# A down projection as seven block products: ten of eleven weight chunks multiplied by blocks, weights streamed by block, angle tables moved to DRAM

## The chip, the cores and the metric

The kernel runs on one core of one Trainium2 chip. The metric is the device time of one execution in microseconds; the time of a kernel is the median over its runs. A core has five engines that run side by side, each with its own in-order queue: TensorE (PE in the profile, its weight loads PEld), VectorE (DVE), ScalarE (ACT), GpSimd (POOL) and SyncE (SP), which only issues transfers (DMAs) and waits. An engine waits at an instruction until the semaphores that it needs have arrived, and all that stands behind it on that engine waits too.

## The reference, cut to what matters

Four layers follow each other on 2048 rows of 512 numbers, all in fp32. Layer 0 is a feed-forward with experts, layer 2 attention over a paged cache, layer 3 a short mix at the end. The change lies in layer 1, apart from a table that layer 2 uses. With `x` the result of layer 0, `F` = 1376 and rank 16, layer 1 computes:

```python
def lora_add(base, inp, A, B):          # a low-rank part for each sequence, of rank 16
    t = einsum('bri,bni->bnr', A[ids], inp)
    return base + einsum('bor,bnr->bno', B[ids], t) * 0.5

gate = lora_add(x @ W_gate.T, x, A_gate, B_gate)     # 512 -> 1376
up   = lora_add(x @ W_up.T,   x, A_up,   B_up)
act  = silu(gate) * up
down = lora_add(act @ W_down.T, act, A_down, B_down) # 1376 -> 512, this product changes
x = x + adapters(down)                               # a base product and gated adapters
```

Layer 2 rotates queries and keys by angles: `cos(pos * freq)` and `sin(pos * freq)`, for each of the 2048 positions 64 numbers.

## The kernel before, in words

The kernel is written in a tile framework: the code names tiles and operations, and the framework sets semaphores, hands out buffers and puts the instructions of each engine in an order. A tile name with `bufs=n` has n buffers; a new tile of that name waits until the readers of the tile n before it are done. Where the code wants an order of its own it adds edges:

- `on_pe` ties each matmul to the one before it, so TensorE's order is that of the program.
- `load_by` ties each of its loads on SP to the one before it, so these loads too go out in program order. An entry that waits for a buffer or for data holds up all that follow.
- the gathers of layer 1 (`gather`, on POOL) are put behind `last_sum`, the last store of a weight sum.

Layer 1 goes over eight groups of 256 rows (two tiles of 128). A group has two phases. First come the *features*: gate and up for eleven chunks of F, ten of 128 and one of 96 (`FC`, `NFC` = 11). They are already computed as seven block products in place of eight (`p1` to `p7`), on sums of the weights and sums of x, with matmuls of 128 columns. `seconds` adds the low-rank part, two chunks at a time, and `finish` makes `actT` on ACT and DVE. In chunk f, `p7(f)` puts a product into the accumulator `acc_a`, DVE reads it at line 587, and `p4(f)` then overwrites it, so TensorE waits for that read.

Second comes the *down phase*: `down` multiplies the eleven chunks of `actT` by `down1T`, four matmuls of 256 columns for each chunk. The down tiles are loaded by `next_down`, seven ahead (`AHEAD`); a product frees a buffer for the tile seven further. Between chunks ten and eleven stand the low-rank products `low` (for the next group, `low_ps`) and `low_down` (`low_d_ps`). Two copies, on ACT and DVE, bring the result `pz` to `zT`, which the adapters (`choose`, `base`, `out`) use during the features of the next group.

Beside this POOL prepares layer 2: `all_sums` yields pairs of functions. `rows` loads four blocks of a weight matrix (`blocks`, two buffers) through `load_by`; `add` makes four sums of them on POOL and stores them to DRAM. Layer 2 reads them as weights of its own block products. Each group makes five sums, one function for each feature chunk (`parts`).

So SP's program order in a group is: rows of the first two sums (chunks 0 and 2), then `load_firsts` for the low-rank weights of down and of the next group's x (16 loads, and register loads ahead of each eight), rows of the third sum, the seven down tiles, the x of the next group, rows of the last two sums, and in the down phase the remaining down tiles. The next group's x is turned by TensorE in the last feature step, just ahead of the down phase.

`rotary_tables` makes cos and sin once, while layer 0 runs, and keeps both in SBUF (4 KB of each partition apiece) up to the end of layer 2, where POOL multiplies them with norm weights in `tables`.

Of the kernel before, what the change touches and what calls it, by code (L numbers as in the profile page):

```python
# [24 lines left out]
F32 = mybir.dt.float32  # L25
I32 = mybir.dt.int32
U32 = mybir.dt.uint32
AF = mybir.ActivationFunctionType
ALU = mybir.AluOpType
# [4 lines left out]
P = 128  # L34
B, S, D = 64, 32, 512
NT = B * S // P
# [4 lines left out]
F1 = 1376  # L41
FC = [(o, min(P, F1 - o)) for o in range(0, F1, P)]

# [308 lines left out]
def sum_up(c, pool, blocks, dst):  # L352


    nc = c.nc
    w = []

    def rows():
        w.append(pool.tile([P, 4, D // 2], F32, name="blocks", bufs=2))
        for n, block in enumerate(blocks):  # L360
            c.load_by(w[0][:, n, :], block)

    def add():
        t = pool.tile([P, 4, D // 2], F32, name="sums")
        (b11, b12, b21, b22), (t1, t2, t3, t4) = ([v[:, n, :] for n in range(4)] for v in (w[0], t))
        nc.gpsimd.tensor_tensor(t1, b12, b11, ALU.subtract)
        nc.gpsimd.tensor_tensor(t3, b22, b12, ALU.subtract)
        nc.gpsimd.tensor_tensor(t2, b22, t1, ALU.subtract)
        nc.gpsimd.tensor_tensor(t4, b21, t2, ALU.subtract)
        c.last_sum = nc.gpsimd.dma_start(dst, t).ins  # L370

    return rows, add
# [10 lines left out]
def all_sums(c, pool, sums):  # L383

    a, H = c.a, D // 2
    for h in range(HALVES):
# [14 lines left out]
def layer1(c, kp, x_in, x_out, sums):  # L401
# [14 lines left out]
    AHEAD = 7  # L416
    with ExitStack() as ctx:
# [34 lines left out]
        class Group:  # L452
            def __init__(self, g):
                self.g = g
                self.h, self.po = [None] * G, [None] * G
                self.a, self.b, self.c, self.part, self.first, self.wd = {}, {}, {}, {}, {}, []
# [166 lines left out]
            def next_down(self, f):  # L623

                if f < NFC:
                    w = FC[f][1]
                    t = wdp.tile([P, D], F32, name="down1T")
                    c.load_by(t[:w], a["down1T"][f * P:f * P + w])
                    self.wd.append(t)

            def down(self, fs, last):
                if 0 in fs:
                    self.pz = [ps.tile([P, 2, N], F32, tag=tag, bufs=2, name="pz") for tag in "ab"]
                for f in fs:
                    w, wd = FC[f][1], self.wd.pop(0)
                    for m in range(KC):
                        product(self.pz[m // 2][:, m % 2, :], wd[:w, m * P:(m + 1) * P],
                                self.actT[:w, f, :], m % 2 == 0 and f == 0, False)
                    self.next_down(f + AHEAD)
                if not last:  # L640
                    return
                for m in range(KC):
                    product(self.pz[m // 2][:, m % 2, :], self.B["Bd1"][:, m * P:(m + 1) * P],
                            self.low_d[:, 0, :], False, m % 2 == 1)
                self.zT = gp.tile([P, KC, N], F32, name="zT")
                nc.scalar.copy(self.zT[:, 0:2, :], self.pz[0])
                nc.vector.tensor_copy(self.zT[:, 2:4, :], self.pz[1])
# [61 lines left out]
        wB = c.load(wp, "B1", [P, D], a["B1"])  # L709
        nb_thr = c.row(wp, "b_thr1")  # L710
# [25 lines left out]
        for g, new in enumerate(groups):  # L736
            old = groups[g - 1] if g else None
            then = groups[g + 1] if g + 1 < len(groups) else None
            parts = [f for _ in range(5) for f in next(to_sum)]

            def features(f):
# [9 lines left out]
                if f:  # L751
                    new.p4(f - 1)
                    if f % 2:
                        new.seconds(f - 1, False)
                        if f < NFC:
                            new.seconds(f, True)
                    new.finish(f - 1)
                if f < NFC:
                    new.p6(f)
                    new.p3(f)  # L760
                if g == 0:
                    sums_of(f + 2)
                if f < len(parts):
                    parts[f]()
# [33 lines left out]
            new.down(range(NFC - 1), False)  # L798
# [4 lines left out]
            new.down((NFC - 1,), True)  # L803
# [10 lines left out]
def rotary_tables(c, pool, scratch):  # L814
# [12 lines left out]
    tables = []  # L827
    for name, turn in (("cos", 0.25), ("sin", 0.0)):
# [4 lines left out]
        r = scratch.tile([P, NT, half], F32, name="rest")  # L833
# [4 lines left out]
        t = pool.tile([P, NT, half], F32, name=name)  # L838
        nc.scalar.activation(t, r, AF.Sin)
        tables.append(t)  # L840
    return tables


class Known:


    def __init__(self, c, kp):
        tc, nc, a = c.tc, c.nc, c.a
        half = HD // 2
        with tc.tile_pool(name="l2_setup", bufs=1) as scratch:  # L850
            self.cos, self.sin = rotary_tables(c, kp, scratch)
# [34 lines left out]
def attention(c, known, x_in, y_part, y_out, sums, tail):  # L886
# [18 lines left out]
    with ExitStack() as outer:  # L905
# [8 lines left out]
        cos, sin, rows, lens = known.cos, known.sin, known.rows, known.lens  # L914
# [110 lines left out]
        class Projections:  # L1025
# [10 lines left out]
            def load(self):  # L1036
                self.xt = [c.load(xp, "xt", [P, D], x_in(T), bufs=2) for T in self.T]

            def tables(self, n):
                for i, T in enumerate(self.T):  # L1040
                    ct = qp.tile([P, 2, half], F32, name=n + "_cos")
                    st = qp.tile([P, 2, half], F32, name=n + "_sin")
                    for t, w_n, f in ((ct, norm[n][0], cos), (st, norm[n][1], sin)):
                        self.last_pool = nc.gpsimd.tensor_tensor(
                            t, w_n, f[:, T, :].unsqueeze(1).to_broadcast([P, 2, half]), ALU.mult).ins
# [672 lines left out]
def emit(tc, a, layers=(0, 1, 2)):  # L1718
    with ExitStack() as ctx:
# [11 lines left out]
        for n in layers:  # L1731
# [3 lines left out]
            if n != 0 and n == next(m for m in layers if m):  # L1735
# [3 lines left out]
                known = Known(c, kp)  # L1739
                sums = {}  # L1740
                for h in range(HALVES):
# [95 lines left out]
```

## Time and profile before

| | us |
|---|---|
| median of 3 runs (3495.23 to 3498.11) | 3495.39 |
| the profiled execution, device time | 3498.47 |
| its span, first to last instruction | 3496.7 |
| TensorE busy in it | 3432.7 (98%) |
| DVE / ACT / POOL busy in it | 2124.5 / 1554.7 / 1617.2 |
| features of group 0, then its down phase | 376.8 to 423.6, to 447.2 |
| features of a later group (602.7 to 657.6), its down phase | 54.9, 23.4 |

Layer 0 ends and layer 1 begins near 374 us of the span, layer 1 ends near 1006, layer 2 near 3327.

How the views are read: a timeline row has the start in us, the length in us, the engine, the line of the kernel, the operation, output<-inputs by the program's names, the shape and the count of merged instructions; in brackets stands how long the engine had been idle before and what released it. A matmul in fp32 shows as two records. `SPq` is SP's queue of transfers; the length is that of the issue, not of the transfer. Matmuls overlap, so their pace is the distance of starts and not the length.

### The profile page before, as it was taken

What the parts mean: (1) busy time and instruction counts of PE and PEld (TensorE: products, weight loads), DVE (VectorE), ACT (ScalarE), POOL (GpSimd) and SP (SyncE); (2) the same over time, 40 slices, a digit from 0 to 9 for tenths busy, and PEclk for the clock granted to TensorE, in tenths of its full rate; (3) what the DMA queues carried; (4) which work ended last, traced back from release to release, by engine and by line L of the source; (5) the groups of instructions that cost most, each with busy time, mean ns of one, the idle gap of its engine ahead of it and who ended that gap; (6) DMA issues with size and microseconds to landing.
All of it is one profiled execution on the core that took longest, in us unless ns stands there. A gap on an engine that the chain in (4) does not pass through costs nothing. (4 is left out here: it accounts for less than half of the span.)

```text
span 3496.7 us, 65764 instructions
## 1 busy us (share of the span) xinstructions
PE 3432.7 (98%) x20736; PEld 2601.2 (74%) x20736; DVE 2124.5 (61%) x5284; ACT 1554.7 (44%) x4089; POOL 1617.2 (46%) x1606
## 2 busy tenths in 40 slices
PE   8999999999999999999999999999999999999999
PEld 4445788888856778777787787777877778778755
DVE  4443534434457676766767767677676676766433
ACT  4111222222226555655555555555565555555411
POOL 0112432323336645645556455465564655644232
PEclk9999999999999999999999999999999999999999
DMA  6013454544466788888878888878888788887721
GB/s 220 25 34 126 159 168 154 168 151 157 139 202 213 239 261 251 259 258 256 257 249 258 255 250 258 262 251 267 256 260 262 247 267 250 259 259 241 228 85 58
DMA packets 630635, 736.00 MB, mean 210 GB/s; under 512 B 64274, under 2 KB 480018, under 8 KB 630290
## 3 DMA queue, kind: packets, MB, share of 16 engines
q1 hardware_dynamic: 577810, 558.74, 51.4%
q0 software_dynamic: 50176, 168.86, 13.9%
q8 instruction: 168, 2.75, 0.3%
q10 hardware_dynamic: 2304, 4.20, 0.3%
q14 instruction: 177, 1.45, 0.1%
HBM read 689.61 MB, written 41.94 MB: 209 GB/s over the span
## 5 line engine op out<-in xcount | busy, mean ns | idle before, releaser
L957 POOL DMA_INDIRECT vt<-in_v_rows,v_rows x512 | 512.5, 1001 | 304.9 <-PE po L931 178.7
L1220 ACT ACTIVATE pr<-pr,low 128x544 f32<-128x544 f32 x512 | 383.3, 749 | 532.3 <-DVE low L1218 486.0
L1213 PE MATMUL sc<-kt,qT 128*128 128x288 f32 (+1 forms) x2048 | 555.5, 394 | 8.1 <-DVE low L1218 6.5
L931 PE MATMUL po<-prT,vt 128*128 128x128 f32 x4096 | 544.9, 276 | 7.4 <-ACT prT L1231 5.9
L931 PEld LDWEIGHTS po<-prT,vt 128*128 128x128 f32 x4096 | 522.7, 192 | 39.1 <-ACT prT L1231 19.0
L1213 PEld LDWEIGHTS sc<-kt,qT 128*128 128x128 f32 x2048 | 385.1, 190 | 223.1 <-issue 123.0
L1218 DVE CUSTOM_DVE_ANT_0 pr<-sc,mask 128x544 f32<-128x544 f32 x512 | 368.2, 719 | 139.3 <-PE sc L1213 101.5
L1005 POOL TENSOR_TENSOR projected<-projected,swapped 128x512 f32<-128x512 f32 x160 | 208.4, 1302 | 300.9 <-DVE projected L1004 277.8
L1225 DVE TENSOR_SCALAR pr<-pr,low 128x512 f32<-128x512 f32 x512 | 315.3, 616 | 12.8
L926 PE MATMUL prT_ps<-ident,pr 128*128 128x128 f32 x2048 | 311.7, 275 | 2.6 <-DVE pr L1225 2.4
L1231 ACT COPY prT<-prT_ps 128x512 f32<-128x512 f32 x512 | 294.0, 574 | 35.2 <-PE prT_ps L926 20.1
L1222 DVE RECIPROCAL low<-low 128x1 f32<-128x1 f32 x512 | 82.0, 160 | 312.8 <-ACT pr L1220 245.7
L926 PEld LDWEIGHTS prT_ps<-ident,pr 128*128 128x128 f32 x2048 | 237.4, 142 | 11.8 <-issue 3.8
L931 PE MATMUL py<-wo,oT 128*128 128x256 f32 x1024 | 241.8, 379 | 0.0
L931 PE MATMUL pq<-wp,x_sums 128*128 128x512 f32 x512 | 240.8, 593 | 0.9 <-issue 0.5
L931 PEld LDWEIGHTS py<-wo,oT 128*128 128x128 f32 x1024 | 186.5, 190 | 21.1
L130 POOL TENSOR_TENSOR rs<-rs,minus_half 128x4 f32<-128x4 f32 x160 | 181.0, 1131 | 22.5 <-DVE low L1222 14.9
L931 PE MATMUL pq<-wp,xT 128*128 128x512 f32 x384 | 182.0, 597 | 3.9 <-DVE projected L1091 3.9
L931 PE MATMUL py<-wo,o_sum 128*128 128x256 f32 x768 | 181.4, 380 | 4.4 <-DVE o_sum L1149 2.5
L1223 ACT ACTIVATE own_pr<-pr,low 128x32 f32<-128x32 f32 x512 | 164.9, 322 | 46.2 <-DVE low L1222 37.4
L1006 POOL TENSOR_TENSOR projected<-projected,rs 128x512 f32<-128x512 f32 x160 | 172.4, 1078 | 7.9
L964 ACT COPY own_vt<-v 32x128 f32<-32x128 f32 x512 | 150.8, 295 | 54.9 <-PE po L931 42.4
(283 smaller groups left out, 6197.7 us busy)
## 6 DMA issues: line engine op xcount, KB each, us to landing
kt<-in_kT SPq DMA_DIRECT2D x2048, 64.0 KB
wp<-in_sums SPq DMA_DIRECT2D x192, 512.0 KB
wo<-out_sums SPq DMA_DIRECT2D x128, 512.0 KB
wp<-in_WqT SPq DMA_DIRECT2D x96, 512.0 KB
wo<-in_WoT SPq DMA_DIRECT2D x96, 512.0 KB
down1T<-in_down1T SPq DMA_DIRECT2D x80, 256.0 KB
wp<-in_WkT SPq DMA_DIRECT2D x32, 512.0 KB
xt<-x SPq DMA_DIRECT2D x48, 256.0 KB
```

What stands on the lines that cost most here:

```text
L130: self.nc.gpsimd.tensor_tensor(t, t, self.minus_half[:, :n], ALU.pow)
L926: c.on_pe(nc.tensor.transpose(pt[:, m, :], piece, c.ident))
L931: c.on_pe(nc.tensor.matmul(out, lhsT, rhs, start=first and i == 0, stop=last and i == len(pairs) - 1))
L957: nc.gpsimd.indirect_dma_start(out=vts[b % 2][:, n, :], out_offset=None, in_=a["v_rows"], in_offset=bass.IndirectOffsetOnAxis(ap=rows[h][: ...
L1005: nc.gpsimd.tensor_tensor(src, src, tmp, ALU.add)
L1006: nc.gpsimd.tensor_tensor(src, src, rs.unsqueeze(2).to_broadcast([P, REP, HD]), ALU.mult)
L1213: c.on_pe(nc.tensor.matmul(sc[:, lo + n * PSIZE:lo + m * PSIZE].rearrange("p (n k) -> p n k", k=PSIZE), q, kt[:, n:m, g, :], start=True, s ...
L1218: nc.vector.tensor_tensor_reduce(pr[:, :NK], sc[:, lo:lo + NK], masks[h, b], -SCALE, 3.0e38, ALU.add, ALU.min, low[:, 0:1])
L1220: nc.scalar.activation(pr[:, :NK], pr[:, :NK], AF.Exp, bias=low[:, 0:1], scale=-1.0, accum_out=low[:, 1:2])
L1223: nc.scalar.activation(own_prs[b % 2][:, g * S:(g + 1) * S], pr[:, L:NK], AF.Copy, scale=low[:, 2:3])
L1225: nc.vector.tensor_scalar(pr[:, :L], pr[:, :L], low[:, 2:3], None, ALU.mult)
L1231: last_prT.append(nc.scalar.copy(prT, pt).ins)
```

## The change

The first ten chunks of the down product become a 2x2 block product by the same scheme as the features: the K side is cut into chunks 0 to 4 and 5 to 9 (`FB` = 5), the rows into the two tiles of the group, the 512 outputs into two halves. Each half again is made in two steps `u` of 128 outputs. For each `u` seven products of five chunks, with 128 columns each, take the place of eight; the order is `DOWN`. Four of the seven use sums of the weights, which `all_sums` now makes first and stores to `down_sums` in DRAM: five more sums, all in group 0, which makes ten where the others make five. Four sums of activations are made on DVE after `finish` of chunks 5 to 9 (`act_sums`). The weights of a product are one tile of five blocks of 128x128, 14 tiles a group, five ahead. The eleventh chunk (`wd_last`, now loaded once) and the low-rank part are added in `down_rest`, which also makes `zT` out of the blocks. To fit in SBUF, `blocks` has one buffer instead of two, and the angle tables go to DRAM, from where layer 2 loads 64 KB for each tile of rows.

```diff
     def rows():
-        w.append(pool.tile([P, 4, D // 2], F32, name="blocks", bufs=2))
+        w.append(pool.tile([P, 4, D // 2], F32, name="blocks"))
...
 def all_sums(c, pool, sums):
     a, H = c.a, D // 2
+    for f in range(FB):
+        yield sum_up(c, pool, [a["down1T"][at * P:(at + 1) * P, n * H:(n + 1) * H] for at in (f, f + FB)
+                               for n in range(2)], sums["down"][:, f])
...
-    AHEAD = 7
+    AHEAD = 5
+    DOWN = (1, 5, 6, 7, 2, 3, 4)
...
+            def act_sums(self, i):
+                x11, x21 = (self.actT[:, i, t * P:(t + 1) * P] for t in range(2))
+                x12, x22 = (self.actT[:, i + FB, t * P:(t + 1) * P] for t in range(2))
+                if i == 0:
+                    self.s = gp.tile([P, 4, FB, P], F32, name="act_sums")
+                s1, s2, s3, s4 = (self.s[:, n, i, :] for n in range(4))
+                nc.vector.tensor_tensor(s1, x21, x22, ALU.add)
+                nc.vector.tensor_tensor(s2, s1, x11, ALU.subtract)
+                nc.vector.tensor_tensor(s3, x11, x21, ALU.subtract)
+                nc.vector.tensor_tensor(s4, x12, s2, ALU.subtract)
+
+            def next_down(self, i):
+                if i < 2 * len(DOWN):
+                    u, m = i // len(DOWN), DOWN[i % len(DOWN)]
+                    t = wdp.tile([P, FB, P], F32, name="down1T")
+                    if m in (1, 2, 3):
+                        k, n = {1: (0, 0), 2: (1, 0), 3: (1, 1)}[m]
+                        at = (2 * n + u) * P
+                        src = a["down1T"][k * FB * P:(k + 1) * FB * P, at:at + P].rearrange("(f p) n -> p f n", p=P)
+                    else:
+                        src = sums["down"][:, :, {5: 0, 6: 1, 7: 2, 4: 3}[m], u * P:(u + 1) * P]
+                    c.load_by(t, src)
                     self.wd.append(t)
...
+            def down(self, u, ms):
+                lo, hi = slice(0, FB), slice(FB, 2 * FB)
+                for m in ms:
+                    if m in (1, 2):
+                        t = ps.tile([P, D], F32, tag="a" if m == 1 else "b", bufs=2, name="pz")
+                        self.pz[u, m == 2] = t.rearrange("p (n c) -> p n c", n=4)
+                    x = {1: self.actT[:, lo, :P], 2: self.actT[:, hi, :P], 4: self.actT[:, hi, P:],
+                         3: self.s[:, 3], 5: self.s[:, 0], 6: self.s[:, 1], 7: self.s[:, 2]}[m]
+                    at, w = {1: 0, 6: 1, 7: 2, 5: 3, 2: 0, 3: 1, 4: 2}[m], self.wd.pop(0)
+                    for f in range(FB):
+                        product(self.pz[u, m in (2, 3, 4)][:, at, :], w[:, f, :], x[:, f, :],
+                                m in (1, 2) and f == 0, f == FB - 1, more=m not in (1, 2))
+                    self.next_down(u * len(DOWN) + DOWN.index(m) + AHEAD)
+
+            def down_rest(self, u):
+                pz = self.pz[u, True].rearrange("p (t n) c -> p t n c", t=2)
+                w = FC[-1][1]
+                for n in range(2):
+                    q = slice((2 * n + u) * P, (2 * n + u + 1) * P)
+                    for lhsT, rhs in ((wd_last[:w, q], self.actT[:w, NFC - 1, :]), (self.B["Bd1"][:, q], self.low_d[:, 0, :])):
+                        product(pz[:, :, n, :], lhsT, rhs.rearrange("p (t c) -> p t c", t=2), False, True, more=True)
...
+                pa, v = self.pz[u, False], tp.tile([P, 5, P], F32, name="pz_sums", bufs=1)
+                nc.scalar.copy(v[:, 0], pa[:, 0])
+                nc.vector.tensor_tensor(v[:, 4], pa[:, 1], v[:, 0], ALU.add)
+                nc.vector.tensor_tensor(v[:, 2], pa[:, 2], v[:, 4], ALU.add)
+                nc.vector.tensor_tensor(v[:, 1], pa[:, 3], v[:, 4], ALU.add)
+                nc.vector.tensor_tensor(v[:, 3], pa[:, 3], v[:, 2], ALU.add)
+                nc.vector.tensor_tensor(self.zT.rearrange("p (n m) (t c) -> p m t n c", n=2, t=2)[:, u], pz,
+                                        v[:, :4].rearrange("p (t n) c -> p t n c", t=2), ALU.add)
...
-            parts = [f for _ in range(5) for f in next(to_sum)]
+            parts = [f for _ in range(5 if g else 5 + FB) for f in next(to_sum)]
...
                     new.finish(f - 1)
+                    if FB <= f - 1 < 2 * FB:
+                        new.act_sums(f - 1 - FB)
...
-                if f < len(parts):
-                    parts[f]()
+                for part in parts[:1 if g else 2]:
+                    part()
+                del parts[:1 if g else 2]
...
-            new.down(range(NFC - 1), False)
+            new.down(0, DOWN)
             if then:
                 then.x_sums()
                 then.low()
             new.low_down()
-            new.down((NFC - 1,), True)
+            new.down(1, DOWN[:4])
+            new.down_rest(0)
+            new.down(1, DOWN[4:])
+            new.down_rest(1)
...
-def rotary_tables(c, pool, scratch):
+def rotary_tables(c, scratch, dst):
...
-        t = pool.tile([P, NT, half], F32, name=name)
-        nc.scalar.activation(t, r, AF.Sin)
-        tables.append(t)
-    return tables
+        nc.scalar.activation(r, r, AF.Sin)
+        nc.sync.dma_start(dst[:, :, m, :], r)
...
                 self.xt = [c.load(xp, "xt", [P, D], x_in(T), bufs=2) for T in self.T]
+                self.angles = [c.load(xp, "angles", [P, 2, half], known.angles[:, T], bufs=4) for T in self.T]
```

## The prediction

> **What bounds the kernel now.** I read the page first, then TensorE's timeline over one steady layer-1 group, then the queue of SyncE (SP) and GpSimd (POOL) in the first group, then VectorE (DVE) beside one pair of feature chunks.
>
> ```profile
> span 3496.7 us, 65764 instructions
> PE 3432.7 (98%) x20736; PEld 2601.2 (74%) x20736; DVE 2124.5 (61%) x5284; ACT 1554.7 (44%) x4089; POOL 1617.2 (46%) x1606
> ```
>
> TensorE is busy 98% of the span: what shortens its own work shortens the kernel, and what makes it wait lengthens it by the whole wait. Its order is written out by hand (on_pe), so nothing can fill a hole.
>
> ```profile
> 579.08 17.43 PE L450 MATMUL pz<-actT,down1T 128*128 128x256 f32 x80
> 596.44 1.27 PE L450 MATMUL low_ps<-xT,first_x 128*32 128x64 f32 x64
> 597.52 1.65 PE L450 MATMUL low_d_ps<-actT,first_down 128*32 128x64 f32 x88
> 599.10 1.99 PE L450 MATMUL pz<-actT,down1T 96*128 96x256 f32 x8
> 600.93 1.89 PE L450 MATMUL pz<-low_d,Bd 128*128 128x256 f32 x8
> 602.66 0.61 PE L450 MATMUL acc_a<-xT,gate1T 128*128 128x128 f32 x4
> 603.10 0.61 PE L450 MATMUL acc_c<-x_sums,sums_gate_up 128*128 128x128 f32 x4
> ```
>
> The first column is the start, and from start to start is the pace. Each fp32 matmul of the code is two records. The ten full chunks are 40 matmuls in 17.36 us, 0.434 each with 256 columns; a run of four records with 128 columns takes 0.447, so 0.2236 a matmul. The down phase runs from 579.08 to 602.66, 23.6 us, with no wait. There are eight such groups.
>
> ```profile
> 376.98 0.33 SPq L102 DMA_DIRECT2D blocks<-in_WkT  x1
> ...
> 384.19 0.43 SPq L102 DMA_DIRECT2D blocks<-in_WvT  x1
> 388.76 5.41 SPq L102 DMA_DIRECT2D first_down<-in_A1down  x8
> 398.55 5.15 SPq L102 DMA_DIRECT2D first_x<-in_A1x  x8
> 403.80 0.37 SPq L102 DMA_DIRECT2D blocks<-in_WkT  x1
> ...
> 405.63 3.29 SPq L102 DMA_DIRECT2D down1T<-in_down1T  x7
> 408.96 0.91 SPq L102 DMA_DIRECT2D xt<-x  x2
> ...
> 425.50 5.51 SPq L102 DMA_DIRECT2D down1T<-in_down1T  x4
> ```
>
> This is group 0 on SP. load_by keeps these loads in program order, and the rows show that order: two sums' blocks, the low-rank firsts, a third sum's blocks, seven down tiles, the next x, later the other down tiles. SP passes each in time only because it rarely has to wait for POOL, which consumes the blocks:
>
> ```profile
> 384.67 0.73 POOL L366 TENSOR_TENSOR sums<-blocks 128x256 f32<-128x256 f32 x1 [5.81 <-DMA blocks<-in_WvT]
> 393.20 0.72 POOL L366 TENSOR_TENSOR sums<-blocks 128x256 f32<-128x256 f32 x1 [4.22 <-DMA in_sums<-sums]
> ```
> ```profile
> 668.75 0.72 POOL L366 TENSOR_TENSOR sums<-blocks 128x256 f32<-128x256 f32 x1 [7.28 <-DMA blocks<-in_WvT]
> 675.48 0.74 POOL L366 TENSOR_TENSOR sums<-blocks 128x256 f32<-128x256 f32 x1 [2.66 <-DMA in_sums<-sums]
> ```
>
> From one sum's first add to the next with nothing else in the way: 8.5 us while the queues are full, 6.7 later. A sum is a slow thing, and the change moves sums in front of TensorE's weights.
>
> **The change, part by part.**
>
> *Down products.* Removed: 17.36 us a group. Added: 2 output pairs x 7 products x 5 chunks = 70 matmuls at 0.2236 = 15.65. The eleventh chunk and the low-rank part stay 8 matmuls of 256 columns, 3.56 us (599.10 to 602.66), only split over u. Gain 1.71 us a group, 13.7 over eight.
>
> *Ten sums in group 0, one block buffer.* Group 0 now makes 10 sums instead of 5 (parts is 5 + FB, two parts per feature chunk), the five of down first, and blocks has one buffer: rows of sum k+1 wait on SP until the adds of sum k are done, and everything behind them on SP waits too. The next SP entries are, in order: rows 0 to 2, firsts, rows 3 and 4, down tiles 0 to 4, the next x, rows 5 to 9, down tiles 5 to 13. Tile 1 is product 5's, read from the sums in DRAM, so it waits for the store of sum 4. One sum now costs: adds 2.95 (668.75 to the end of L369), then either the store (0.3, 0.8 and 2.7) or the reload (first add 2.85 after the first issue, as from 456.96 to 459.81, and 0.4 more for the fourth block). Both give 6.3 to 6.8; I take 6.8. Then, in span time:
> - sums 0, 1, 2 start at 384.7, 391.5, 398.3; rows 2 are issued by 396.2.
> - The firsts take SP 19.2 us (384.5 to 403.7 before, register loads included): 415.4. Sum 3 starts at 418.3, sum 4 at 425.1, its adds end at 428.1 and its store has landed at 431.7.
> - SP issues tiles 1 to 4 and x until 434.3. The x tiles come behind 1.3 MB of weights; with 222 GB/s at a DMA share of 0.67 in this phase before (331 at full), they land at about 438.5. TensorE transposes this x before the down phase, at 420.58 before, so it stands from there: about 18 us.
> - It then needs 3.0 us to the down phase (420.58 to 423.58) and 5.6 for products 0 to 4: 447, a microsecond or two more after the idle time.
> - Rows 5 go out at 434.3, behind the same traffic: sum 5 at 440, sums 6 to 8 at 446.8, 453.6, 460.4, rows 9 until 465.1, tile 5 issued then and landed at 468.5. TensorE stands a second time, over 20 us.
> - What is left of the phase: 9 products 10.1, low_ps 1.1, low_d 1.6, the rests 3.6, together 16.3, and 2.0 for the clock: after the idle time at the handover of layers low_ps took 1.94 (374.86 to 376.80) against 1.08 later, and the next twelve records lost another 1.2. End 486.8, against 447.2: **+39.6 us**, group 0's own saving in it. With 6.3 a sum and tile 5 sooner it is +33, with 8.5 as at the start +50.
>
> The gathers for group 1 are put behind the last sum on POOL: about 472 to 477, wanted by the second chunk of that group near 495, so covered.
>
> In groups 1 to 7 the same queue has five sums over 78 us: the last block loads were issued by 636.4 before and slip by one sum, to about 643, while tile 5 is wanted at 658.7. That cover is 15 us, and I cost the single buffer there at nothing. Without the cover each sum too many would cost 6.8.
>
> *Sums of activations.* 20 VectorE adds of 128x128 a group. Nearest rows: 128x256 in SBUF 0.42, 128x128 from PSUM 0.29. [...]
>
> ```profile
> 569.10 0.42 DVE L621 SCALAR_TENSOR_TENSOR actT<-sg,up 128x256 f32<-128x256 f32 x1
> 569.63 0.29 DVE L587 TENSOR_TENSOR up<-acc_a,p 128x128 f32<-128x128 f32 x1
> 571.15 0.29 DVE L614 TENSOR_TENSOR gate<-acc_b,p 128x128 f32<-128x128 f32 x1 [1.23 <-PE acc_b L450]
> ```
>
> If they run after L587 they fit the hole of 1.23. If they run after L621 and ahead of L587, L587 ends at 571.1 and p4, which started at 570.09, waits about 0.9. The other chunks of a pair have 0.3 to 0.6 of slack more. Three such chunks in a group: 0 to 2.7 us, 0 to 19 over seven groups (in group 0 it hides under the queue). DVE's order in the trace is by readiness, not by program (L616 before L615), so I take a third: +6.
>
> *Weights by block.* 14 tiles of 328 KB a group instead of 11 of 256, in rows of 512 bytes instead of 2 KB, the first five ahead, nine in the phase. TensorE eats one in 1.118 us, 293 GB/s while a run of products lasts; low_ps, low_d and the rests give 6.2 us of rest in it, and the two large gathers (1.4 MB) fall into its first 6 us. At the 331 GB/s above, 2.95 MB and the gathers take 13 us of some 18. [...] Bounds 0 and +21, I take +1. The trace has no down load with 512-byte rows, so the upper end stays in the range.
>
> *Tail of the product.* Six instructions make the blocks into zT. The first five of each pair need only products 1, 5, 6, 7 and run under products 2, 3, 4; the last one (128x512 with PSUM, 0.69 like L647) takes the place of the copies L646 and L647, 0.59 and 0.69, and has the first chunk of the next group (2.2 us) over it. Nothing; without that cover 0.7.
>
> *Angles.* Two DMAs on SP and Sin in place in layer 0, where DVE made these tables between 256 and 271 while TensorE had no wait; 32 loads of 64 KB in attention, two pairs of tiles ahead, 14 us of SP issues over 2300. Only the first, at the handover near 1006, has little cover. 0 to +3, I take +1. The single load of the last rows goes with the other weights of layer 1: nothing.
>
> Sum: 39.6 - 7 x 1.71 + 6 + 1 + 1 = **+36**. The profiled execution took 3498.5 with a span of 3496.7, 3.1 over the median of the runs, 3495.4. On the median: 3531.
>
> **The rivals.**
>
> *The queue keeps up.* If SP got past rows 5 to 9 by 425, or a sum took under 3 us, nothing stands in group 0: -13.7 plus 0 to 8 for DVE, DMA and angles, 3482 to 3490. For it: down tiles were never waited for before. Against it: the adds alone are 2.95 a sum, so nine sums before tile 5 need 27 us with no load or store at all, and with them 57 to 61, where only 40 are there. This is the faster side; it decides at about 4.5 us a sum.
>
> *Stalls that eat the gain, and no more.* Half the queue's price, 20 us, is still more than the gain; for no change group 0 may lose some 6 to 12 us, so tile 5 would have to land by about 438. Little speaks for it: 3490 to 3500.
>
> *A stall in every group.* The weights come late (+21) or DVE stands ahead of p4 each time (+19): 3545 to 3556. For it: 293 GB/s is near what the queues reach; against it: the rests between the products.
>
> **How the numbers follow.** The queue in group 0 as worked out, 0.74 (3531, from 3512 with short sums and no other stall to 3545); a stall in every group besides, 0.10; the queue keeps up, 0.11; no change, 0.05. The range 3508 to 3554 leaves out the faster cases and the far end. A difference under 0.2% (7 us) can't be told from none here. Faster 0.11, same 0.05, slower 0.84.
>
> **What would show it.** In the timeline of the changed kernel: group 0's down phase ending near 487 instead of 447; TensorE idle twice in it, the first before xt's transpose, the second before a product of the third block, with a DMA named; SP waiting for POOL's L369 between block loads, 6 to 7 us apart; 15.65 us for the 14 products of a later group, which then is 1.7 shorter from group to group. L587 as releaser of acc_a in more than six places would show DVE's part. The prediction is wrong if SP issues down tiles 5 to 13 before 440, or if later groups stand for weights.

## The result and the profile after

The changed kernel takes 3582.09 us (median, 3579.13 to 3586.27), and the kernel before, run beside it, 3496.75 (3495.23 to 3505.24). The ratio is 1.0239, with a 95% interval of 1.0225 to 1.0252: slower by 85 us. The forecast was slower by 36, between 13 and 59.

The head of the page of the changed kernel:

```profile
span 3581.9 us, 67124 instructions
PE 3441.3 (96%) x21216; PEld 2621.3 (73%) x21216; DVE 2186.9 (61%) x5516; ACT 1551.9 (43%) x4097; POOL 1639.3 (46%) x1631
```

TensorE's busy time even rose by 9 us (time at a slow clock counts as busy: from 564.58 to 566.00 it is busy for 1.42 us at a granted clock of 0.50), but its share fell from 98% to 96%: most of the 85 us is idle time. Where it lies, the waits of TensorE between 370 and 1120 us say (what it worked on, what released it: total, times, longest):

```profile
PE pz L455 <- DMA down1T<-in_down1T: 30.9, 6, 25.0
PE xT_ps L491 <- DMA xt<-x: 22.6, 1, 22.6
PE pz L455 <- DMA down1T<-down_sums: 14.4, 8, 3.2
PE acc_a L455 <- DVE up L592: 7.9, 18, 1.0
```

In the kernel before, none of the first three existed, and the last was smaller:

```profile
PE acc_a L450 <- DVE up L587: 2.5, 6, 0.7
```

Two single waits of 25.0 and 22.6 us are group 0. The other thirteen waits for down1T, 20.3 us together, lie in the later groups.

**Group 0.** TensorE's timeline there:

```profile
443.30 1.11 PE L491 MATMUL xT_ps<-ident,xt 128*128 128x128 f32 x4 [22.56 <-DMA xt<-x]
...
478.07 2.50 PE L455 MATMUL pz<-act_sums,down1T 128*128 128x128 f32 x10 [24.98 <-DMA down1T<-in_down1T]
...
497.58 0.60 PE L455 MATMUL pz<-low_d,Bd 128*128 128x256 f32 x2
```

The phase ends at 498.0; before, it ended at 447.2. SP's queue beside it:

```profile
418.32 8.23 SPq L103 DMA_DIRECT2D blocks<-in_down1T  x8
426.61 0.52 SPq L103 DMA_DIRECT2D down1T<-in_down1T  x1
435.22 2.14 SPq L103 DMA_DIRECT2D down1T<-down_sums  x3
...
438.09 1.43 SPq L103 DMA_DIRECT2D xt<-x  x2
439.62 0.38 SPq L103 DMA_DIRECT2D blocks<-in_WkT  x1
...
448.71 0.33 SPq L103 DMA_DIRECT2D blocks<-in_WkT  x1
...
464.00 0.33 SPq L103 DMA_DIRECT2D blocks<-in_WkT  x1
...
473.16 1.02 SPq L103 DMA_DIRECT2D down1T<-in_down1T  x1
```

The next x, issued at 408.96 before, goes out at 438.09; the sixth weight tile waits at 473.16 for the rows of the tenth sum. From the first block loads of one sum to those of the next it is 7.4 to 9.1 us (between 448.71 and 464.00 lie those of one more sum), the period of a sum on POOL.

**A later group.** The down phase of group 1, and the same on SP:

```profile
554.11 1.28 PE L455 MATMUL pz<-actT,down1T 128*128 128x128 f32 x10
555.22 3.51 PE L455 MATMUL pz<-act_sums,down1T 128*128 128x128 f32 x30
558.57 1.28 PE L455 MATMUL pz<-actT,down1T 128*128 128x128 f32 x10
561.96 1.38 PE L455 MATMUL pz<-act_sums,down1T 128*128 128x128 f32 x10 [2.10 <-DMA down1T<-in_down1T]
564.58 2.50 PE L455 MATMUL pz<-actT,down1T 128*128 128x128 f32 x10 [1.24 <-DMA down1T<-down_sums]
567.01 1.94 PE L455 MATMUL low_ps<-xT,first_x 128*32 128x64 f32 x64
568.73 2.26 PE L455 MATMUL low_d_ps<-actT,first_down 128*32 128x64 f32 x88
570.92 1.38 PE L455 MATMUL pz<-actT,down1T 128*128 128x128 f32 x10
```
```profile
555.42 0.38 SPq L103 DMA_DIRECT2D down1T<-in_down1T  x1
556.53 0.53 SPq L103 DMA_DIRECT2D down1T<-down_sums  x1
```

Five products run at the pace that was forecast, 1.118 each, and then the blocks ahead are used up. The sixth product (554.11 + 5 x 1.118 = 559.7) finds its tile, issued at 555.42, not there until 561.96, and the seventh waits again. From 564.58 ten records take 2.43 us from start to start instead of 1.12: the granted clock is 0.50 from 563.55 to 570.38. The phase lasts 28.19 us instead of 23.58, 3.3 of it waits.

Split by stage, from start to start in the two timelines (a down phase ends where the next features begin; the group of the table before that starts at 602.7 has, by its rows, 54.6 and 23.6 and not 54.9 and 23.4):

| | before | after | difference |
|---|---|---|---|
| group 0, end of the down phase | 447.2 | 498.0 | +50.9 |
| features of groups 1 to 7 | 380.7 | 390.2 | +9.5 |
| down phases of groups 1 to 7 | 164.2 | 185.4 | +21.1 |
| from layer 1's last product to the end | 2504.6 | 2508.3 | +3.7 |
| span | 3496.7 | 3581.9 | +85.2 |

### The profile page after: what moved, and what is told of

Same layout as the page of the kernel before. It is cut to its first block, busy times and chain, and to the rows that moved or that the text cites. A ratio compares the mean times of both kernels' runs of the same rounds, so it can differ in the third digit from the quotient of the medians.

```text
span 3581.9 us, 67124 instructions
## 1 busy us (share of the span) xinstructions
PE 3441.3 (96%) x21216; PEld 2621.3 (73%) x21216; DVE 2186.9 (61%) x5516; ACT 1551.9 (43%) x4097; POOL 1639.3 (46%) x1631
## 5 line engine op out<-in xcount | busy, mean ns | idle before, releaser
L1271 DVE TENSOR_SCALAR pr<-pr,low 128x512 f32<-128x512 f32 x512 | 297.4, 581 | 12.8
L367 POOL TENSOR_TENSOR sums<-blocks 128x256 f32<-128x256 f32 x45 | 32.8, 728 | 376.5 <-DMA blocks<-in_WoT 117.0
```

Source lines behind the costliest of these rows:

```text
L1271: nc.vector.tensor_scalar(pr[:, :L], pr[:, :L], low[:, 2:3], None, ALU.mult)
```

## The experiments

In each stage a theory stood against rivals. The theory after the result: group 0 loses by SP's queue, as forecast; the later phases lose since the gathers for the next group take the transfers' first 6 us (1.00 of 1.34 MB from 554 to 560 us) while only 5.6 us of products are ahead; the features lose by VectorE. The rivals: rows of 512 bytes, the queues' rate over the whole phase, the single block buffer. Each kernel is read by the table of stages that follows; a single profile's time moves by some us in the part behind layer 1 (2498.8 to 2510.7 in the table), which none of the edits but the angles touches.

| kernel | group 0: features, down | features, mean of groups 1 to 6 | down, mean of 1 to 7 | behind layer 1 | span |
|---|---|---|---|---|---|
| before | 46.8, 23.6 | 54.46 | 23.46 | 2504.6 | 3496.7 |
| after | 70.5, 50.8 | 55.98 | 26.48 | 2508.3 | 3581.9 |
| e1_no_down_sums | 46.8, 29.6 | 56.08 | 26.13 | 2502.2 | 3528.8 |
| e2_five_then_six | 67.4, 25.7 | 56.60 | 26.82 | 2505.0 | 3555.1 |
| e3_no_gathers | 71.4, 49.3 | 56.03 | 22.42 | 2501.7 | 3547.5 |
| e4_wide_rows | 71.7, 49.3 | 56.18 | 24.89 | 2501.0 | 3564.1 |
| e5_act_sums_late | 71.3, 50.2 | 55.84 | 26.84 | 2498.8 | 3572.8 |
| e6_angles_alone | 46.7, 23.6 | 54.51 | 23.45 | 2503.3 | 3495.9 |
| e7_one_block_buffer | 47.3, 23.6 | 54.44 | 23.45 | 2510.7 | 3502.0 |
| e8_gathers_later | 71.5, 49.5 | 56.02 | 23.41 | 2506.8 | 3559.4 |
| e9_all_mended | 60.9, 23.8 | 56.46 | 22.73 | 2500.9 | 3514.0 |
| e10_mended_adds_on_pool | 46.4, 27.6 | 55.37 | 27.38 | 2510.1 | 3537.1 |
| e11_mended_adds_on_dve | 45.6, 25.8 | 56.34 | 24.89 | 2508.4 | 3522.2 |
| e12_six_ahead | 71.9, 47.6 | 55.86 | 23.56 | 2503.4 | 3552.3 |

**No sums of down.** The weights' sums are not made; products of sums read plain blocks.

```diff
-    for f in range(FB):
+    for f in range(0):
         yield sum_up(c, pool, [a["down1T"][at * P:(at + 1) * P, n * H:(n + 1) * H] for at in (f, f + FB)
...
-            parts = [f for _ in range(5 if g else 5 + FB) for f in next(to_sum)]
+            parts = [f for _ in range(5) for f in next(to_sum)]
...
-                for part in parts[:1 if g else 2]:
+                for part in parts[:1]:
```

> The changed kernel without the sums of the down weights: all 14 tiles are read from down1T itself, in the same 512-byte rows, and group 0 makes five sums as before. Left out: the weight sums, so four of the seven products have the wrong weights; the instructions of TensorE and the bytes of the tiles stay. Queue theory (SP behind POOL's sums is what group 0 lost): group 0's down phase ends at 447 to 452 instead of 498, neither the wait before xT_ps (22.6) nor the one of 25.0 is there, span near 3531. Rival (the 512-byte tiles or the sums' share of the queues cost group 0 its time): the waits stay in part, span over 3555. Later groups keep their 27 to 28 us down phases under either.

Measured: 3530.55, group 0's features at 46.8 as before. The two long waits are gone. A wait of 4.97 for the sixth tile is left, since rows of the fourth and fifth sum still stand ahead of it on SP. So the queue carries group 0, and nothing of it touches the later groups, whose phases stay at 26.1. The edit takes away two things, the five sums and the second part in each chunk; the mended kernels below tell them apart.

**Five sums in group 0, six in each later group.** All products and all sums are kept; the five others are only moved.

```diff
-            parts = [f for _ in range(5 if g else 5 + FB) for f in next(to_sum)]
+            parts = [f for _ in range(6 if g else 5) for f in next(to_sum, ())]
```

> The changed kernel with only the five down sums in group 0 and six sums in each later group, in place of ten and five: the rows of sums 5 to 9 no longer stand ahead of down tile 5. Queue theory: the second wait of group 0 (25.0 before tile 5) goes, the first (22.6, x behind tile 1, which waits for sum 4's store) stays within 2 us, span 3582 - 27 = 3555. Rival (one long stall that only moves, since the sums have to be made anyway): the wait comes back in group 1 or before the first tile, span over 3572.

Measured: 3556.84. The wait for tile six falls from 24.98 to 1.50, and of the one for x 17.94 of 22.56 stay (within 2 us was expected):

```profile
439.26 1.12 PE L491 MATMUL xT_ps<-ident,xt 128*128 128x128 f32 x4 [17.94 <-DMA xt<-x]
451.20 1.38 PE L455 MATMUL pz<-act_sums,down1T 128*128 128x128 f32 x10 [1.50 <-DMA down1T<-in_down1T]
```

The two waits thus belong, in the main, to two halves of the ten sums: the five of down, put in two parts to a chunk, hold x; the five of attention hold the sixth tile.

**No gathers in the down phase.** The gathered low-rank rows are fetched once, for group 0, and used by all groups; the other gathers are left out.

```diff
             if then:
-                then.load_seconds()
+                then.B = new.B
                 then.x(1)
```

> The changed kernel without the gathers of Bg, Bu and Bd from group 1 on (each group uses the low-rank rows of group 0, so those are of the wrong sequences): 1.66 MB less in front of down tiles 5 and 6 of each group. Theory (the five tiles ahead cover 5.6 us, and the gathers hold the transfer engines for the first 4 to 5): the waits before products 5 and 6 go and the down phases of groups 1 to 6 fall from 27 to 28 to about 22, span near 3582 - 33 = 3549; group 0 is unchanged at 50.8. Rival (rows of 512 bytes are too slow by themselves): down phases stay over 26 and the span over 3570.

Measured: 3549.26. The later phases take 22.35, 23.57, 22.58, 21.96, 21.95 and 21.96 in groups 1 to 6, with no wait for a weight (two of them have waits of 1.46 and 0.36 for which the profile names nothing). The removed term and the added one are as computed: 15.65 us for 70 matmuls, and the rest as before, make 21.9. Group 0 is as in the changed kernel.

**Weight blocks in rows of 2560 bytes.** The plain blocks come from a copy of the weights laid out by block, and the sums are stored by block, so that a tile is one row of 2560 bytes for each partition instead of five of 512.

```diff
-                        src = a["down1T"][k * FB * P:(k + 1) * FB * P, at:at + P].rearrange("(f p) n -> p f n", p=P)
+                        at = ((k * 2 + n) * 2 + u) * P
+                        src = a["down1B"][at:at + P, :].rearrange("p (f n) -> p f n", n=P)
                     else:
-                        src = sums["down"][:, :, {5: 0, 6: 1, 7: 2, 4: 3}[m], u * P:(u + 1) * P]
+                        src = sums["down"][:, {5: 0, 6: 1, 7: 2, 4: 3}[m], u]
```

> The changed kernel with the same blocks laid out in DRAM so that each partition's part of a tile is one row of 2560 bytes instead of five of 512 (down1T in a second, blocked copy; down_sums in another order of dimensions, its stores in rows of 512). Row theory: the down phases of groups 1 to 6 fall to about 22, span near 3549. Gather theory: a tile saves about a quarter of its 1.16 us, the gathers stay in front of it, so the down phases fall by 1 to 2.5 us each only, span 3567 to 3576.

Measured: 3565.89, phases of 24.9 instead of 26.5. By this one profile the rows are about a third of the stall (1.6 of the 4.5 us that lie between 26.5 and 21.95), the gathers the larger part. For the forecast's 1.16 us and its quarter, the transfer records of the changed kernel from 500 to 1000 us: on the queue of SP's loads a packet of 512 bytes takes 29.3 ns in the mean and one of 2048 bytes 86.6, so a tile of 640 packets on 16 engines takes 1.17 us, as an estimate, and a quarter less at the rate of the larger packets.

**The gathers later.** They wait for the seventh product of the phase.

```diff
             if then:
-                then.load_seconds()
                 then.x(1)
             new.down(0, DOWN)
             if then:
+                then.load_seconds(c.last_pe)
                 then.x_sums()
...
+            if after:
+                tc.add_manual_dep(ins.ins, after, mybir.DependencyInfo(
+                    mybir.DependencyClass.Sync, mybir.DependencyReason.DATA), reason="gather in the down phase")
```

> The changed kernel, with the three gathers for the next group made to wait for the last of the first seven products of the down phase; nothing is left out. If the gathers at the head of the phase hold up the weight tiles behind them (products 5 and 6 waited 2.1 and 1.2 us in most groups), the later down phases fall from 27 to 28.5 to 22 to 23.5 us, as without gathers: about 3550. Rival, tiles come late wherever the gathers lie: the wait moves to the second seven products, or to the next group's second chunk, which needs the gathered rows, and the time is 3565 to 3580.

Measured: 3561.19, phases of 23.4, nearer to the theory than to its rival: the same gathers, later in the phase, give back two thirds of the stalls. Waits of 0.2 to 1.4 for a tile stay in some groups, and one phase of 25.6 has a wait of 1.79 for which the profile names nothing (more on these behind the next run).

**Six blocks ahead instead of five.** The gathers, the rows and the bytes are those of the changed kernel.

```diff
-    AHEAD = 5
+    AHEAD = 6
```

> The changed kernel with six weight blocks ahead instead of five; nothing is left out. If the later down phases stand because the blocks ahead are eaten (5 x 1.118 = 5.6 us) before the tiles that queue behind the gathers have landed, one more block covers 1.1 us of each phase's 3.3 us of waiting, and some of the half clock behind it: 25 to 26.5 us instead of 27.2 to 28.3, together 7 to 14 us less, 3568 to 3575. Group 0 stays, since its seventh tile still goes out behind the last sum's rows. Rival, the queue's rate over the whole phase is the limit: a tile ahead only moves the wait to a later product, and the phases stay at 27 to 28.

Measured: 3554.08. The phases of groups 1 to 7 fall to 23.6 in the mean, those of groups 4 to 6 to 21.95, with no wait in them. Group 6 in TensorE's timeline:

```profile
952.08 1.28 PE L455 MATMUL pz<-actT,down1T 128*128 128x128 f32 x10
953.20 3.51 PE L455 MATMUL pz<-act_sums,down1T 128*128 128x128 f32 x30
956.55 1.28 PE L455 MATMUL pz<-actT,down1T 128*128 128x128 f32 x10
957.67 1.28 PE L455 MATMUL pz<-act_sums,down1T 128*128 128x128 f32 x10
958.78 1.28 PE L455 MATMUL pz<-actT,down1T 128*128 128x128 f32 x10
959.99 1.26 PE L455 MATMUL low_ps<-xT,first_x 128*32 128x64 f32 x64
```

Seven products in a row from 952.08; in the changed kernel group 6 waited 2.57 and 0.83 here. In these groups the rate over the whole phase is not the limit: one tile of nine is moved ahead of the phase, the first of the others may land 1.1 us later, and all arrive in time. Groups 1 to 3 did in part what the rival said: their wait moved to the seventh product (2.14, 1.49 and 2.07 us), and the phases took 25.85, 27.66 and 24.50. Why they differ from groups 4 to 6 was not tested. The gain, 20.5 us over seven phases, is larger than expected; 30 records of the second seven products take 3.35 us from start to start in these phases, at 1.118 for ten, but for group 2 (4.87, from 649.50) and group 3 (3.56, from 730.91).

Group 2 has a second wait, behind two records of a product whose tile had landed:

```profile
641.88 1.38 PE L455 MATMUL pz<-actT,down1T 128*128 128x128 f32 x10 [1.49 <-DMA down1T<-down_sums]
648.40 1.31 PE L455 MATMUL pz<-actT,down1T 128*128 128x128 f32 x8 [2.05 <-issue]
```

"issue" says that the profile names no releaser. The transfer records name a candidate: a transfer of 16 KB on queue q8, of the kind "instruction" on the page, landed at 646.85, and TensorE went on at 648.40. The kernels in the table have 16 single waits of this kind in layer 1 (from 380 us on), of 0.26 to 2.48 us, and each ends 1.1 to 1.6 us after such a transfer has landed. So TensorE may have waited for its own program; no run tests it.

**The adds of activations later.** They are emitted after the next chunk's `p7`, whose result DVE must read before `p4`.

```diff
                     new.finish(f - 1)
-                    if FB <= f - 1 < 2 * FB:
-                        new.act_sums(f - 1 - FB)
...
                 if f:
                     new.p7(f - 1)
+                    if FB <= f - 2 < 2 * FB:
+                        new.act_sums(f - 2 - FB)
```

> The changed kernel, with the four sums of activations of a chunk emitted after the next chunk's p7 and its DVE read of acc_a instead of right after finish; nothing is left out. Order theory: the features of groups 1 to 6 grew from 54.5 to 56 us because these adds stand ahead of that read (18 waits of acc_a for DVE, 7.9 us, against 6 and 2.5 before). Then the waits fall back to about 6 and the features to 54.5 to 55, some 9 us over the groups: about 3573. Rival, the single block buffer or the traffic makes the features longer: they stay at 56, and the time at 3582.

Measured: 3574.56, which looks like the order theory's 3573 and is not. The features are 55.84 instead of 55.98, and L592 is still named for 6.6 us of waits for acc_a, 13 times. The missing 9 us lie behind layer 1 (2498.8 against 2508.3), where this edit does nothing. Nor did it do what it was made for: in the trace VectorE's order is not that of the program, and the adds (L635) stand ahead of the read (L592) as they did.

```profile
535.38 0.70 DVE L635 TENSOR_TENSOR act_sums<-actT 128x128 f32<-128x128 f32 x1
535.99 0.28 DVE L592 TENSOR_TENSOR up<-acc_a,p 128x128 f32<-128x128 f32 x1
```

In the changed kernel the same two rows stand at 535.84 and 536.46. Of its waits for L592 in the features of groups 1 to 7, all 11 of over 0.2 us have L635 directly ahead of the read; here 9 of 10 have. So this run leaves the order theory untested.

**The angle tables alone**, in the kernel before (the diff's part on `rotary_tables`, `Known`, `load` and `tables`, nothing of layer 1).

```diff
-        t = pool.tile([P, NT, half], F32, name=name)
-        nc.scalar.activation(t, r, AF.Sin)
...
+        nc.scalar.activation(r, r, AF.Sin)
+        nc.sync.dma_start(dst[:, :, m, :], r)
```

> The kernel before, with the angle tables in DRAM alone; nothing is left out. The changed kernel took 3.7 us more from the end of layer 1 to the end than the kernel before, in one profile each. If the loads of the angles cost that (the first one at the handover near 1006 above all), this kernel is 2 to 4 us slower than before. If it is the spread of single runs, as the prediction had it: 0 to +1 us.

Measured: 3494.98 (10 runs) against 3491.04 (13), a ratio of 1.001, interval 1.0 to 1.0019, that is 0 to 6.6 us. The part behind layer 1 took 2503.3 in its profile, 2504.6 before; over all profiles of the table it lies between 2498.8 and 2510.7 and follows no edit. The angles cost something between nothing and 6.6 us; the 3.7 of the two profiles is no measure of it.

**One block buffer alone**, in the kernel before.

```diff
-        w.append(pool.tile([P, 4, D // 2], F32, name="blocks", bufs=2))
+        w.append(pool.tile([P, 4, D // 2], F32, name="blocks"))
```

> The kernel before, with one buffer for the blocks of a weight sum instead of two and nothing else. As the prediction has it, later groups lose nothing by it (15 us of cover): features 54 to 55 and down phases 23.6 as before, span within 3 us of before's 3496.7. In group 0 the third sum's rows now wait for the second's adds, ahead of the down tiles and the next x: there it may cost 0 to 10 us. Rival: the single buffer is what made the features of the changed kernel 1.5 us longer, and they are 55.5 to 56 here too.

Measured: 3503.79 (the kernel before, beside it, 3500.09), with features of 54.4 and phases of 23.5 in the later groups as before, and 47.3 instead of 46.8 in group 0. The buffer costs half a microsecond with five sums in a group.

**All mended**, three times. Group 0 multiplies by plain chunks and makes the five sums of down; later groups make six sums; gathers, rows and adds are emitted as in the runs above. The second and third kernels also go back to one part of a sum for each feature chunk in group 0, and the second has the adds of activations on POOL:

```diff
-                for part in parts[:1 if g else 2]:
+                for part in parts[:1]:
...
-                nc.vector.tensor_tensor(s1, x21, x22, ALU.add)
+                nc.gpsimd.tensor_tensor(s1, x21, x22, ALU.add)
```

> All causes taken away at once, nothing left out: group 0 multiplies by ten plain chunks as before and only makes the five sums of down; groups 1 on make six sums each until all are made; gathers after the first seven products; adds of activations after the next p7; weight blocks in rows of 2560 bytes. If the three causes are all there is, group 0 costs what it did (447.2), the later down phases take 22 to 23 us instead of 23.6 and their features 54.5 to 55.5: 3 to 10 us less than before, 3486 to 3494. Rival: something that moves with the seven products costs as much again (six sums in a group, the loads of the angles, 3.7 us after layer 1): 3497 to 3505, no gain or slower.

> The mended kernel, with one part of a sum per feature chunk in group 0 too (the first mended kernel still did two, and stood 13.9 us before xt's transpose there) and the sums of activations on GpSimd instead of VectorE; nothing is left out. If the two for each chunk hold x back, group 0's features fall from 60.9 to 47; if VectorE's amount of work (35 us busy in 55, 28.5 before) makes the features of the other groups 56.1 instead of 54.5, they fall to 54.5 to 55. Both: 3491 to 3497 on the scale where before is 3491 and the first mended kernel 3518. Rival, GpSimd is late with these sums or slows VectorE: features at 56, or waits before the products of act_sums, 3500 to 3506.

> The same as the one with the sums of activations on GpSimd, but these on VectorE; nothing is left out. Group 0 as there (features 47), the other features at 56 as in the first mended kernel: about 3504 where before is 3491. If it is no slower than the one on GpSimd, VectorE's amount of work is not what makes the features longer.

Measured: 3518.38 (ratio to before 1.0077, interval 1.006 to 1.0094), 3538.26 (1.0112, 1.0094 to 1.0131) and 3526.58 (1.0079, 1.0062 to 1.0096); the kernel before took 3491.04 beside the first and 3500.09 beside the others. None beats it, and all three are slower than theory and rival expected.

- The first stood 13.85 us for x in group 0, because it still put two parts in each chunk. With one part this wait is gone (features of 46.4 and 45.6), as expected.
- The adds on POOL take the features to 55.37, those on VectorE to 56.34. So these adds on VectorE, by their amount or by their place in its order, are a half of what the features gained over 54.46; the other half stays open. POOL then comes late with them: in the phases of groups 2, 4 and 5 products wait for `act_sums` (0.55 to 1.29 us at a time) and then run slower (22 records in 3.92 to 4.19 us from start to start, where 1.118 for ten makes 2.46), and this kernel is the slowest of the three. Group 2:

```profile
591.29 4.35 PE L460 MATMUL pz<-act_sums,down1T 128*128 128x128 f32 x22 [0.98 <-POOL act_sums L640]
```

- The second and third show something more in the down phases: 25.5 us in groups 1 to 6 of the third, with no wait for a weight of over half a microsecond. TensorE stands five times for about 0.4 us amid the low-rank products, and the profile names no releaser ("issue"):

```profile
676.69 1.30 PE L460 MATMUL low_ps<-xT,first_x 128*32 128x64 f32 x50
678.38 0.35 PE L460 MATMUL low_ps<-xT,first_x 128*32 128x64 f32 x5 [0.39 <-issue]
679.13 0.37 PE L460 MATMUL low_ps<-xT,first_x 128*32 128x64 f32 x5 [0.39 <-issue]
```

The products and their order are those of the first mended kernel, whose phases take 22.7. No instruction transfer lands at a fixed distance before these waits; what they are stays open.

What is left to win is small. With the third kernel's group 0 (71.4), features of 55.4 (386 over the seven groups) and phases of 21.95, layer 1 would end, as an estimate from these rows, near 376.6 + 71.4 + 386 + 154 = 988, against 992.1 before; the angles may take those 4 us back. A kernel with all of these was not run, and the features of 55.4 come from the kernel in which POOL was late with the adds.

## Why the prediction was right or wrong

Slower was right, and so was the mechanism of the largest term. The time missed by 51 us and lay outside the range. By its own steps, each against the stages above:

- **Down products, -12 in groups 1 to 7**: right. A phase without waits takes 21.95 instead of 23.58, 1.63 a group against the 1.71 that was taken off.
- **Ten sums in group 0, +39.6**: the mechanism right (TensorE stands for x first, then for a tile of the third block, while SP waits between the sums), the size +50.9. A sum took 7.7 us (its first adds on POOL stand at 445.73 and, four sums on, at 476.35), not 6.8. Adds and issue were as taken; the term that was mis-sized is the store's landing, 2.5 us once and then 3.4 to 3.9 where 2.7 was taken (the idle time of POOL, as in these rows):

```profile
461.10 0.71 POOL L367 TENSOR_TENSOR sums<-blocks 128x256 f32<-128x256 f32 x1 [3.55 <-DMA in_sums<-sums]
468.46 0.71 POOL L367 TENSOR_TENSOR sums<-blocks 128x256 f32<-128x256 f32 x1 [3.43 <-DMA in_sums<-sums]
```

  The first sum's period was 8.8, as the prediction's row of the first sums before had shown (8.5). So x landed at 443.3 and not 438.5, tile six at 478.1 and not 468.5; what followed took 19.9 instead of 18.3. The text had this as the far end: 8.5 a sum, +50.
- **Weights by block, +1**: this is the step that failed. Stalls and the half clock behind them cost +32 (the phases' +21.1, and the 11 us that the products should have gained). The step compared bytes with time over the whole phase, 13 us of 18. The question was the first 6 us. There the gathers take most of what the transfer engines move, before and after alike; this is the transfers' part of the kernel before, from 579 to 585 us:

```profile
q0 software_dynamic: 211, 1.07, 61.2%
q1 hardware_dynamic: 130, 0.24, 14.8%
```

  The columns are packets, MB and share: of 1.31 MB the gathers' queue moved 1.07, and only 0.24 are tiles and other loads of SP; in the changed kernel, from 554 to 560, the gathers moved 1.00 of 1.34. Before, it cost nothing, because seven chunks ahead lasted 7 x 1.736 = 12.2 us. The change cut AHEAD to five and made each tile last 1.118: 5.6 us. That number stood ready in the prediction's own rows and was not put beside the gathers, which it named. No run shows the 21 us of the step's upper bound, which the price of the third rival uses too; the runs showed +32 in its place, and with six blocks ahead tiles that come in time in groups 4 to 6. In the rows above both queues move bytes in the same six microseconds, in unequal parts. The prediction's own sign of being wrong, later groups that stand for weights, came true.
- **The half clock** was priced at 2.0 us in group 0 and nowhere else. It came in groups 1 to 4 and 6 too: a granted clock of 0.50 for 6.83 us in group 1 and for 3.41 in each of the others.
- **Sums of activations, +6**: +9.5, in its bounds. The +6 was worked out with 0.29 us an add, four to a chunk: the author's estimate from the row of an add from PSUM, which the kernel before could not show for `act_sums`. In the changed kernel these adds (L635 to L638) took 0.28 to 0.29 in the median and 0.35 to 0.47 in the mean. The mechanism forecast, reads of acc_a late behind the adds, is in the trace: waits for this read (L587, now L592) grew from 2.5 to 7.9 us, +5.4, in 18 places instead of 6. The other 4 us are not explained, and no run moved the adds on VectorE; taking them off it gave back a half of the growth.
- **One block buffer, 0**: right, by the run of it alone. **Angles, +1**: not settled, 0 to 6.6.
- **The rivals.** The queue nearly kept up only where the sums were taken away. A stall in every group had a chance of 0.10 and came true, with group 0's far end besides; its price of 3545 to 3556 stood on a group 0 of +39.6.

Together 50.9 - 11.4 + 32.5 + 9.5 + 3.7 = 85.2.

## What to carry to other kernels

A prefetch is worth its tiles times the time in which the consumer eats one: a faster product, a smaller tile and a shallower queue multiply, here from 12.2 to 5.6 us, and the number must be held against the longest stretch in which something else owns the transfers, not against an average. Work put ahead of others in an in-order queue cost all behind it its whole period here, store and landing included (7.7 us a sum in group 0); move it to where the queue has slack. The time of one run can agree with a theory by chance: split it by stage, and see in the trace that the edit moved what it was to move, before it is taken as proof.

## What the runs showed of the hardware

TensorE's granted clock was half after short waits. In group 1, with waits of 2.10 and 1.24 us and one product between them, it was 0.50 from 563.55 to 570.38 us, and 1.00 before and behind. The columns are the stretch in us, its length, busy time of PE, PEld, DVE, ACT and POOL, the granted clock, the share of the transfer engines and GB/s:

```profile
564.58:570.92 6.34, 6.34 (x163) 6.05 (x163) 0.42 (x1) 0.00 (x0) 0.00 (x0) 0.54 0.55 150
```

In these 6.3 us the slow clock cost 2.6 us besides the waits (the product 2.43 instead of 1.12 from start to start, the two low-rank products 3.91 instead of 2.65).

The length of the waits alone did not decide it. In the kernel without sums of down, group 4 waited longer than group 5 at the same places, and only group 5 went to half clock:

```profile
765.41 1.38 PE L455 MATMUL pz<-act_sums,down1T 128*128 128x128 f32 x10 [1.63 <-DMA down1T<-in_down1T]
768.30 1.38 PE L455 MATMUL pz<-actT,down1T 128*128 128x128 f32 x10 [1.51 <-DMA down1T<-in_down1T]
...
845.54 1.38 PE L455 MATMUL pz<-act_sums,down1T 128*128 128x128 f32 x10 [0.30 <-DMA down1T<-in_down1T]
848.40 2.40 PE L455 MATMUL pz<-actT,down1T 128*128 128x128 f32 x10 [1.48 <-DMA down1T<-in_down1T]
```

The granted clock is 1.00 from 764 to 778 and 0.50 from 848.55 to 851.96. What else decides was not tested.
